# Seven-product down projection: the product of sums first, A11's product in the third bank and copied to two halves, A12's product one step later

## The chip, the cores and the metric

The kernel runs on one core of a Trainium2 chip. The metric is the device time of one execution in microseconds (us), as the median of several runs; lower is better. Before the change it is 731.59 us, the median of three runs (731.53 to 734.29).

The engines are named as in the profile: PE (TensorE, the matmuls), PEld (its weight loads, which run beside the matmuls), DVE (VectorE), ACT (ScalarE), POOL (GpSimd), SP (SyncE, which issues nearly all DMAs). Matmuls write into PSUM, eight banks of 128 partitions by 512 float32; ACT and DVE read the banks.

## The reference

```python
def _L0_cond_ref(x, cond, norm_w, up_w, down_w):      # x (4, 1024, 512), FF = 2048
    scale = cond @ norm_w.T + 1.0
    ms = jnp.mean(x * x, axis=-1, keepdims=True)
    h = x * (scale[:, None, :] * jax.lax.rsqrt(ms + EPS))
    u = h @ up_w.T                                     # (4, 1024, 4096)
    val, gate = jnp.split(u, 2, axis=-1)
    h = val * jax.nn.gelu(gate, approximate=False)
    hq = h + jax.lax.stop_gradient(act_quant(h) - h)   # whole numbers over a scale per token
    wq = down_w + jax.lax.stop_gradient(weight_quant(down_w) - down_w)   # -1, 0, 1 over one scale
    y = hq @ wq.T                                      # the down projection
    return y + x
```

The change touches the last product alone, `hq @ wq.T`: per batch element 1024 tokens by 2048 channels against a 2048 by 512 matrix.

## The kernel before

The four elements of the batch (`b`) go through the kernel one after the other. The up projection of an element runs in 16 slots (`slot`, one for each 128 of the 2048 channels); for `b` of 1 to 3 it is done with seven products in place of eight (`product` at L574, six matmuls of 512 columns each, in the PSUM banks A, B and E). In the slots of element `b`, the quantization of element `b - 1` is done on DVE and ACT by a planner (`Filler`) that spreads its pieces over places x, y and z of each slot, and the down projection of `b - 1` is put into the slots `DOWN`, 10 to 13, one *pair* of token tiles in each: tile `a` of the first half of the tokens and tile `a` of the second half. For `b` of 1 and 2 that makes eight pairs. The pairs 0 to 2 of the element 2 are done after the last slots, in the tail (`old_first`, `old_third` and the calls beside them); so there are eleven pairs in all. The fourth of element 2 and all of the last element use the plain `down_mm`.

A pair (`Pair`, L812) is itself a product of two-by-two blocks, by seven block products of eight matmuls each. The left blocks are A11, A12 (tokens of the first half, channels of the lower and upper half) and A21, A22, each 128 by 1024 in bfloat16, in R. The right blocks B11 to B22 and their sums T1 to T4 lie in `wd8` in fp8. The left sums s1 to s4 are made by DVE: s1 in `sum1` (L827), into the H slot that this slot will fill only later, and then in `sums` (L834 to L836): A21 becomes s3, s2 takes A11's place, s4 takes A12's place. Each may only be written when the product that reads the old block is done.

A block product is `Pair.product` (L839): eight matmuls of 256 columns, into one half of a bank. All matmuls of all pairs carry the line L851; one product is told from another by its place in time. A pair uses three banks of the tag `po`, k1, k2 and k3 (in the tail pair 1 has the banks B, A and E instead). In the order of PE's queue a slot with a pair runs:

- `early`: `first`, that is A11 x B11 into the second half of k1, with a first matmul of 512 columns (`both`), which writes both halves with the same numbers; ACT copies the second half onto the first (L859); s1 x T1 into k3; then A12 x B21 accumulates onto k1's first half. Then DVE's `sums`.
- three to four up products (A, E, B, and A of the slot before),
- `third` (place `mid[0]`): s2 x T2 accumulates onto k1's second half, ACT copies that half to k2's second half (L868), and DVE adds k3 to the output rows (L891, `onto`),
- an up product in E, then `fourth`: s4 x B22 onto k1's second half, s3 x T3 onto k2's second half, the copy L877; DVE adds k1 to the rows, and makes the next pair's s1,
- an up product in A, then `fifth`: A22 x T4 onto k2's first half, and the rows go out.

A matmul that accumulates onto what ACT has written needs an earlier matmul to have marked the place as written. A `po_set` matmul at L1381 does this once, for the bank of k2, before the first pair.

The order on every engine is that of the code (a manual schedule). The semaphores are laid by the tile framework from what each instruction reads and writes.

Of the kernel before, what the change touches and what calls it, by code (L numbers as in the profile page):

```python
# [18 lines left out]
P = 128  # L19
# [31 lines left out]
def glu_quant_kernel(  # L51
# [15 lines left out]
    HALF = D // 2  # L67
# [44 lines left out]
    for n in range(0, P, 32):  # L112
        c = slice(n, n + 32)
# [25 lines left out]
    def s_tile(g):  # L139


        if g >= NJ:
            return SXY[:, (g + 1) % 2]
        return S_more if g % 3 == 2 else SXY[:, g % 3]
# [667 lines left out]
    class Pair:  # L812
# [23 lines left out]
            DVE.tensor_tensor(self.s[4], a12, self.s[2], ALU.subtract)  # L836
            self.s[3] = a21

        def product(self, w, name, bank, half, start, stop, both=False):  # L839


            w = w.rearrange("p (j t) -> p j t", t=P)
            t = w_block(name)
            n = NJ // 2
            for j in range(n):
                m, po = t[:, :, j], bank[:, half * HALF : (half + 1) * HALF]
                po = po.rearrange("p (c o) -> p c o", c=2)
                if both and j == 0:
                    m = m.rearrange("p (y c) o -> p y c o", y=1).to_broadcast([P, 2, 2, P])
                    po = bank.rearrange("p (y c o) -> p y c o", y=2, c=2)  # L850
                PE.matmul(  # L851
                    po, w[:, j], m, start=start and j == 0, stop=stop and j == n - 1,
                    skip_group_check=True,
                )

        def first(self, banks):
            self.banks = k1, _, k3 = banks
            self.product(self.part(0, 0), "B11", k1, 1, True, True, True)
            ACT.copy(k1[:, :HALF], k1[:, HALF:])  # L859
            self.product(self.s[1], "T1", k3, 0, True, True)  # L860
            self.product(self.part(0, 1), "B21", k1, 0, False, True)

        def third(self, xrs, dq):

            k1, k2, k3 = self.banks
            self.xrs, self.dq = xrs, dq
            self.product(self.s[2], "T2", k1, 1, False, True)
            ACT.copy(k2[:, HALF:], k1[:, HALF:])  # L868
            for h in range(2):
                self.onto(h, k3[:, :HALF], slice(HALF, D))  # L870

# [405 lines left out]
    for b in range(1, B):  # L1277
        dve, act = Filler(), Filler()
        gains(b)
        am = am_tile(b - 1)  # L1280
        dq = state[b - 1] = sm.tile([P, 2 * NA], F32, name=f"dq_{b}", tag="dq")
        last_pair = NJ // 2 - 1
        for h in range(2):
            add_pair(
                dve, act, b - 1, last_pair, h, (0, "xz"[h]),
                lambda now, h=h: token_max(b - 1, h, am),
            )
        for h in range(2):
            for cost, f in token_scale(h, am):
                dve.add((1, "x"), cost, lambda now, f=f: f())  # L1290
        add_pieces(dve, act, b - 1, am, PIECES, (2, "x"))
        for i in range(NJ // 2 - 1):
            for h in range(2):
                add_pair(dve, act, b, i, h, (2 * i + 3, "x"))
        steps = {}
        pairs = {}
        if b + 1 < B:
            sc = cond_load_scale(b + 1)
            bring = lambda b=b, sc=sc: cond_bring(b + 1, sc)
            steps[1, "z"] = [(bring, (0.4, 0))]  # L1300
            p0 = b * NJ + 12
            plan = [
                (None, p0, ((6, "z"), (7, "x"), (7, "y"), (9, "y"), (10, "x"), (10, "z"))),
                (p0 + 4, None, ((9, "y"), (10, "x"), (10, "y"), (11, "y"), (12, "x"), (12, "x"))),
                (None, None, ((10, "y"), (11, "x"), (11, "y"), (13, "x"), (13, "y"), (13, "z"))),
                (p0 + 2, p0 + 4, ((9, "z"), (12, "x"), (12, "y"), (14, "x"), (14, "y"), (14, "z"))),
            ]
            for a, (at, nx_at, places) in enumerate(plan):
                def make(a=a, at=at, nx_at=nx_at, b=b):
                    toks[a] = Tokens(b + 1, a, at, nx_at)  # L1310
                    toks[a].load()
                fs = [
                    make,
                    lambda a=a: toks[a].norm(),
                    lambda a=a, sc=sc: toks[a].scale(sc),
                    lambda a=a: toks[a].high(),
                    lambda a=a: toks[a].low(DVE),
                    lambda a=a: toks[a].turn(),
                ]
                costs = ((0, 0), (0, 1.6), (0, 1.5), (0, 2.1), (2.6, 0), (0, 0))  # L1320
                for place, f, c in zip(places, fs, costs):
                    steps.setdefault(place, []).append((f, c))
        for j in range(NJ):
            g = b * NJ + j
            down = b + 1 < B and j in DOWN
            if down:
                pair, a = pairs[j], DOWN[j]
                xrs = [down_load(b - 1, h, a) for h in range(2)]
            early_sums, late_sums = D_SUM_AT.get((b, j), ((), ()))
            left = SLOT_US + PAIR_US * down - OWN_US + 0.4  # L1330
            more = D_SUM_US * len(late_sums) + 0.7 * (j + 1 == min(DOWN) and b + 1 < B)
            left -= D_SUM_US * len(early_sums) + more
            mine = {p: [sum(c[e] for _, c in steps.get((j, p), ())) for e in range(2)] for p in "xyz"}
            left -= sum(mine[p][0] for p in "xyz")
            act_left = {"x": 2.7, "y": 2.2 if down else 1.1, "z": 0}

            def run(p):
                nonlocal left
                for f, _ in steps.get((j, p), ()):
                    f()  # L1340
                if p == "x":
                    cap = min(left, 3.9 - mine["x"][0] - (0 if down else mine["y"][0] + more))
                    left -= cap - dve.run((j, p), cap)
                elif p == "z":
                    left = dve.run((j, p), left)
                if p != "z":
                    act.run((j, p), act_left[p] - mine[p][1])

            def early():
                if down:  # L1350
                    pair.first([po_bank(f"po_{b}_{a}_{n}") for n in range(3)])
                    pair.sums()
                d_sums(early_sums)

            def next_pair():
                if b + 1 < B and j + 1 in DOWN:
                    pairs[j + 1] = Pair(b - 1, DOWN[j + 1])
                    pairs[j + 1].sum1(h_slots(g + 1)[:, 0, 0])

            def more_sums():  # L1360
                next_pair()
                d_sums(late_sums)

            mid = [nothing] * 3
            if j + 1 == min(DOWN):
                mid[0] = more_sums
            if down:
                mid = [lambda: (pair.third(xrs, dq), d_sums(late_sums)), lambda: (pair.fourth(), next_pair()), lambda: (loads(), pair.fifth())]

            def loads():  # L1370
                if NJ + 2 <= g + 2 < B * NJ:
                    s_load_x(g + 2)
                if NJ + 2 <= g + 1 < B * NJ:
                    s_load_y(g + 1)


            def late():
                if b == 1 and j + 1 == min(DOWN):

                    banks = [po_bank(f"po_set_{n}") for n in range(3)]  # L1380
                    PE.matmul(  # L1381
                        banks[1].rearrange("p (a t) -> p a t", t=P),
                        s_tile(g + 1)[:, 0, 0, :P], t_view(b)[:, :, 0, 0, 0, :],
                        start=True, stop=True,
                    )

            if b + 1 == B and j in DOWN and DOWN[j] < 3:
                pairs[DOWN[j]] = Pair(b - 1, DOWN[j])
                places = old_places(DOWN[j])
                pairs[DOWN[j]].sum1(places[0])  # L1390
                pairs[DOWN[j]].sums(*places[1:])
            if j == 4:
                token_turn(b - 1, am)
            if j == 5:
                bring_dq = token_undo(b - 1, dq)
            if j == 6:
                bring_dq()
            if j == NJ - 1:
                get_ready()
            elif b == 1 and j == 0:  # L1400
                get_ready()
            slot(g, lambda: run("x"), lambda: run("y"), lambda: run("z"), early, mid, late)
            if not down:
                loads()
        assert not act.items and not dve.items, (b, dve.items, act.items)
# [162 lines left out]
```

## Time and profile before

| | |
|---|---|
| median of three runs | 731.59 us |
| the profiled execution | 730.43 us |
| its span, first to last instruction | 728.6 us |
| PE busy | 719.9 us (99%) |
| DVE busy | 581.2 us (80%) |
| ACT busy | 396.3 us (54%) |
| POOL busy | 196.1 us (27%) |
| granted TensorE clock | 1.000 |
| L851, matmuls in `po` from R | 448 records, mean 275 ns |
| L868, ACT copy of 128x256 | 11, each 357 ns |

The span is what the profiler saw from the first to the last instruction. The run takes 1.8 us more than that, which lies around the program. The records of matmuls are pipelined: a record of 256 columns lasts 0.27 us, though the next matmul starts about 0.11 us after it. So the time of a product on PE is read from one start to the next, not from the lengths of its records.

The pairs lie in three stretches: 274 to 337 us (pairs 0 to 3 of element 0, in the slots 10 to 13 of `b` = 1), 445 to 508 us (element 1, `b` = 2), and 669 to 696 us (the tail).

### The profile page before, as it was taken

What the parts mean: (1) busy time and instruction counts of PE and PEld (TensorE: products, weight loads), DVE (VectorE), ACT (ScalarE), POOL (GpSimd) and SP (SyncE); (2) the same over time, 40 slices, a digit from 0 to 9 for tenths busy, and PEclk for the clock granted to TensorE, in tenths of its full rate; (3) what the DMA queues carried; (4) which work ended last, traced back from release to release, by engine and by line L of the source; (5) the groups of instructions that cost most, each with busy time, mean ns of one, the idle gap of its engine ahead of it and who ended that gap; (6) DMA issues with size and microseconds to landing.
All of it is one profiled execution on the core that took longest, in us unless ns stands there. A gap on an engine that the chain in (4) does not pass through costs nothing.

```text
span 728.6 us, 10140 instructions
## 1 busy us (share of the span) xinstructions
PE 719.9 (99%) x3661; PEld 358.8 (49%) x3661; DVE 581.2 (80%) x819; ACT 396.3 (54%) x629; POOL 196.1 (27%) x207
## 2 busy tenths in 40 slices
PE   7999999999999999999999999999999999999998
PEld 3544444444444446655444445665444444445744
DVE  7877889975698899788689897787678888755897
ACT  6868876772336674444335676543433665332274
POOL 1379887775100033440000030360020000000100
PEclk9999999999999999999999999999999999999999
DMA  6759999988444654876735646866934555452253
GB/s 236 251 172 303 291 273 249 254 199 230 117 102 102 131 155 130 180 186 159 181 101 103 131 101 174 202 144 163 230 96 102 90 114 104 101 102 89 89 188 115
DMA packets 203982, 117.30 MB, mean 161 GB/s; under 512 B 165382, under 2 KB 174487, under 8 KB 203932
## 3 DMA queue, kind: packets, MB, share of 16 engines
q1 hardware_dynamic: 203642, 116.33, 63.8%
q8 instruction: 28, 0.46, 0.2%
q10 hardware_dynamic: 290, 0.33, 0.1%
q14 instruction: 22, 0.18, 0.1%
HBM read 54.22 MB, written 23.09 MB: 106 GB/s over the span
## 4 chain that ended last, share of the span: by engine, by line
PE 96%; DVE 1%; DMA 1%; ACT 0%; issue 0%; SPq 0%; DVEq 0%
PE A L580 34%; PE E L580 17%; PE pg L595 10%; PE pv L595 10%; PE B L580 9%; PE po L851 8%; PE po_end L800 4%; PE po L800 1%; DMA H<-in_x_dram 1%; DMA SXY<-H 1%; PE po_B L851 0%; PE ptx L941 0%; PE pv L638 0%; DVE R L949 0%; PE pw L323 0%; PE pg L638 0%
## 5 line engine op out<-in xcount | busy, mean ns | idle before, releaser
L580 PEld LDWEIGHTS <-SXY 128*128 128x128 f16 x2016 | 197.2, 98 | 232.3 <-issue 0.6
L580 PE MATMUL A<-R,SXY 128*128 128x512 f16 x1152 | 266.2, 379 | 0.0
L580 PE MATMUL E<-R,SXY 128*128 128x512 f16 x576 | 140.0, 379 | 0.1
L678 DVE SCALAR_TENSOR_TENSOR H<-A,sg,t 128x512 f32<-128x512 f32 x48 | 36.0, 750 | 73.4 <-PE A L580 73.2
L730 POOL PARTITION_ALL_REDUCE am<-R x8 | 14.4, 1794 | 230.7 <-DVE R L716 230.7
L772 DVE TENSOR_TENSOR H<-H,am 128x1024 f32<-128x1024 f32 x64 | 76.2, 1216 | 0.0
L595 PEld LDWEIGHTS <-SXY 128*128 128x128 f16 x486 | 47.5, 98 | 57.4 <-DMA SXY<-H 0.8
L691 ACT ACTIVATE t<-t,sg 128x512 f32<-128x512 f32 x48 | 34.6, 721 | 70.1 <-DVE t L688 69.9
L580 PE MATMUL B<-R,SXY 128*128 128x512 f16 x288 | 70.0, 379 | 0.0
L714 DVE TENSOR_REDUCE gm<-H 128x512 f32<-128x1024 f32 x56 | 69.0, 1232 | 1.0
L595 PE MATMUL pg<-R,SXY 128*128 128x512 f16 x252 | 57.8, 379 | 0.3 <-DMA SXY<-H 0.3
L851 PE MATMUL po<-wd,R 128*128 128x256 fp8e4 (+1 forms) x448 | 56.8, 275 | 0.0
L595 PE MATMUL pv<-R,SXY 128*128 128x512 f16 x234 | 54.4, 379 | 0.0
L851 PEld LDWEIGHTS <-R 128*128 128x128 bf16 (+1 forms) x480 | 47.0, 98 | 12.8
L675 ACT ACTIVATE t<-B,sg 128x512 f32<-128x512 f32 x48 | 33.0, 688 | 36.4 <-PE B L580 36.4
L484 POOL TENSOR_SCALAR ssq<-ssq 128x2 f32<-128x2 f32 x12 | 3.6, 299 | 176.8 <-ACT xt L514 124.1
L658 ACT COPY t<-A 128x512 f32<-128x512 f32 x48 | 28.0, 583 | 39.5 <-PE A L580 39.2
L666 ACT COPY B<-A 128x512 f32<-128x512 f32 x48 | 27.4, 572 | 39.0 <-PE A L580 38.6
L780 ACT ACTIVATE H<-H 128x1024 f32<-128x1024 f32 x38 | 39.9, 1050 | 14.1 <-DVE H L772 14.1
L670 ACT COPY v<-E 128x512 f32<-128x512 f32 x48 | 28.1, 586 | 31.3 <-PE E L580 27.8
L716 DVE TENSOR_TENSOR R<-R,gm 128x512 f32<-128x512 f32 x56 | 41.9, 749 | 1.3
L697 DVE SCALAR_TENSOR_TENSOR H<-v,sg,t 128x512 f32<-128x512 f32 x48 | 36.6, 762 | 7.4 <-ACT t L691 7.4
(207 smaller groups left out, 972.5 us busy)
## 6 DMA issues: line engine op xcount, KB each, us to landing
SXY<-s_dram SPq DMA_DIRECT2D x57, 256.0 KB, 3.2
s_dram<-SXY SPq DMA_DIRECT2D x18, 384.0 KB, 3.3
H<-in_L_cond_up_w_dram SPq DMA_DIRECT2D x13, 512.0 KB, 5.6
SXY<-s_dram SPq DMA_DIRECT2D x39, 128.0 KB, 3.3
xr<-in_x_dram SPq DMA_DIRECT2D x19, 256.0 KB, 3.5
out_dram<-xr SPq DMA_DIRECT2D x19, 256.0 KB, 2.6
H<-in_x_dram SPq DMA_DIRECT2D x8, 512.0 KB, 7.9
R<-in_L_cond_down_w_dram SPq DMA_DIRECT2D x8, 512.0 KB, 7.1
```

Of the source, the lines that this page charges most:

```text
L580: PE.matmul(o, s[:, w, k, :], tv[:, :, c, l, k, :], start=start and n == 0, stop=stop and n == len(TERMS) - 1, skip_group_check=True,)
L595: PE.matmul(ps, a[k // 2][:, w, k % 2, :], XP[:, l, k, h * TOK : (h + 1) * TOK], start=n == 0, stop=n == len(terms) - 1,)
L675: ACT.activation(cur["t1"], pb, AF.Gelu, scale=gain(g, 1))
L678: DVE.scalar_tensor_tensor(h_half(g - 1, 0), prev["A"], gain(g - 1, 0), prev["t1"], ALU.mult, ALU.mult)
L691: ACT.activation(prev["t2"], prev["t2"], AF.Gelu, scale=gain(g - 1, 1))
L697: DVE.scalar_tensor_tensor(h_half(g - 1, 1), prev["v"], gain(g - 1, 0), prev["t2"], ALU.mult, ALU.mult)
L714: DVE.tensor_reduce(gm[0], v, AX.X, ALU.max, apply_absolute_value=True)
L716: return [largest, lambda: DVE.tensor_tensor(m, m, gm[0], ALU.max)]
L772: DVE.tensor_tensor(v, v, r.to_broadcast([P, 2, TOK]), ALU.mult)
L780: ACT.activation(v, v, AF.Copy, bias=MAGIC)
L800: PE.matmul(po.rearrange("p (y c o) -> p y c o", c=2, o=P), q[:, a, h, j], wd8[:, :, j // n, j % n, :, y0:y1].rearrange("p c o y -> p y c o"),
L851: PE.matmul(po, w[:, j], m, start=start and j == 0, stop=stop and j == n - 1, skip_group_check=True,)
```

## The change

`first` makes s1 x T1 first, into k3's first half. Then A11 x B11 goes into k3's second half, which was not used before, with eight matmuls of 256 columns; `both` and its wide matmul are gone. One ACT copy, now of 512 columns, reads this half twice and writes both halves of k1. A12 x B21 leaves `first` and is put in `third`, after s2 x T2 and the copy to k2. As A12 is then still needed when `sums` runs, s4 goes to the other half of the H slot that holds s1 (the tail's pairs had places of their own for their sums already). Before the first pair the `po_set` matmul is done for two banks in place of one.

```diff
-        def product(self, w, name, bank, half, start, stop, both=False):
+        def product(self, w, name, bank, half, start, stop):
...
-                if both and j == 0:
-                    m = m.rearrange("p (y c) o -> p y c o", y=1).to_broadcast([P, 2, 2, P])
-                    po = bank.rearrange("p (y c o) -> p y c o", y=2, c=2)
...
         def first(self, banks):
             self.banks = k1, _, k3 = banks
-            self.product(self.part(0, 0), "B11", k1, 1, True, True, True)
-            ACT.copy(k1[:, :HALF], k1[:, HALF:])
             self.product(self.s[1], "T1", k3, 0, True, True)
-            self.product(self.part(0, 1), "B21", k1, 0, False, True)
+            self.product(self.part(0, 0), "B11", k3, 1, True, True)
+            m1 = k3[:, HALF:].rearrange("p (y o) -> p y o", y=1).to_broadcast([P, 2, HALF])
+            ACT.copy(k1.rearrange("p (y o) -> p y o", y=2), m1)
...
             self.product(self.s[2], "T2", k1, 1, False, True)
             ACT.copy(k2[:, HALF:], k1[:, HALF:])
+            self.product(self.part(0, 1), "B21", k1, 0, False, True)
...
-                    pair.sums()
+                    pair.sums(None, h_slots(g)[:, 0, 1])
...
-                    PE.matmul(
-                        banks[1].rearrange("p (a t) -> p a t", t=P),
-                        s_tile(g + 1)[:, 0, 0, :P], t_view(b)[:, :, 0, 0, 0, :],
-                        start=True, stop=True,
-                    )
+                    for bank in banks[:2]:
+                        PE.matmul(
+                            bank.rearrange("p (a t) -> p a t", t=P),
+                            s_tile(g + 1)[:, 0, 0, :P], t_view(b)[:, :, 0, 0, 0, :],
+                            start=True, stop=True,
+                        )
```

## The prediction

> **What bounds the kernel now.** I read the page first, then who waited for whom, then the timeline around the pairs.
>
> ```profile
> PE 719.9 (99%) x3661; PEld 358.8 (49%) x3661; DVE 581.2 (80%) x819; ACT 396.3 (54%) x629; POOL 196.1 (27%) x207
> ...
> PE 96%; DVE 1%; DMA 1%; ACT 0%; issue 0%; SPq 0%; DVEq 0%
> ```
>
> The second line is the chain that ended last: 96% of the span is PE's queue running one matmul after another. A 99% busy PE alone would prove little, as records overlap. So I took starts: between 264 us and the end only three matmuls start later than their queue would let them, two by 0.2 us (a product in E, 265.7 and 436.8 us) and one in a pair:
>
> ```profile
> PE po L851 <- DVE H L827: 0.6, 1, 0.6
> ```
>
> (who waited for whom, PE alone: total, times, longest). Hence whatever is added to PE's stream in the pairs is added to the end, and whatever is taken out is gained, with hardly any idle time on PE to absorb either.
>
> **The wide matmul (removed).** The first pair, timeline (start us, us, engine, line, operation):
>
> ```profile
> 273.86 0.38 PE L1381 MATMUL po_set<-R,SXY 128*128 128x512 f16 x1
> ...
> 274.07 1.14 PE L851 MATMUL po<-wd,R 128*128 128x512 fp8e4 x8
> ...
> 275.06 1.04 PE L851 MATMUL po<-wd,H 128*128 128x256 fp8e4 x8
> 275.26 0.36 ACT L859 COPY po<-po 128x256 f32<-128x256 f32 x1
> ...
> 275.93 1.04 PE L851 MATMUL po<-wd,R 128*128 128x256 fp8e4 x8
> ```
>
> A11's eight matmuls, one of them wide, take 275.06 - 274.07 = 0.99 us; s1's eight narrow ones 275.93 - 275.06 = 0.87. The change makes the first like the second: -0.11 us (the wide one's extra 256 columns), eleven times, -1.2 us. The second `po_set` costs what the first does: 274.07 - 273.86 = +0.2 us, once.
>
> **The wait that is removed.** A12 x B21 now waits in `first` for the copy L859. Here that copy ends at 275.62 and B21 starts at 275.93, exactly 0.87 after s1's product: the wait is hidden by s1's product and costs nothing. In no pair but one (below) does `first` take longer than its columns. So nothing is gained here. DVE's s4 no longer waits for B21 either; DVE (80%) sets no end, so this is worth nothing by itself.
>
> **The wait that is added.** B21 now stands in PE's queue right behind s2 x T2 and writes k1's first half, while ACT reads k1's second half for the copy to k2. The changed program, as built, lets B21's first matmul in each of the eleven pairs wait for that very copy: the framework keeps two engines apart by bank, though the halves differ. Before, PE went on into bank E:
>
> ```profile
> 283.28 1.04 PE L851 MATMUL po<-wd,R 128*128 128x256 fp8e4 x8
> ...
> 284.15 1.46 PE L580 MATMUL E<-R,SXY 128*128 128x512 f16 x6
> 284.35 0.36 ACT L868 COPY po<-po 128x256 f32<-128x256 f32 x1 [0.29 <-PE po L851]
> ```
>
> From T2's first matmul to the copy's end is 284.71 - 283.28 = 1.43 us; the same in the other pairs I read (298.56 to 299.99, 313.85 to 315.28, 329.90 to 331.33), 1.48 in the tail (673.32 to 674.80). From ACT's end to a matmul that waits for it: at 16.39 us ACT's L349 ends, the load and matmul of L638 start at 16.45, so 0.06. Before, the next matmul came 0.87 after T2's first. The added wait is 1.43 + 0.06 - 0.87 = 0.62 us in a slot, 1.48 + 0.06 - 0.87 = 0.67 in the tail. This supposes that ACT is free when T2 ends. The line view of L868 says so for all eleven copies:
>
> ```profile
>   PE po L851: 6.1, 10
>   PE po_B L851: 0.5, 1
> ```
>
> (what ACT sat idle for before the copy: us, times). So 8 x 0.62 + 3 x 0.67 = **+7.0 us**. Behind the waiting matmul stand B21's other seven, the product in E, then B22 and T3; DVE's sum of E and ACT's Gelu behind them slide with PE. As nothing in PE's queue may pass, nothing covers this. Its lower bound is 0.56 a pair (no hand-over time at all), its upper bound what a late ACT would add; the least idle time before L868 was 0.28 us, so none here.
>
> The Trainium skill ("PSUM — Partial Sum Buffer", section "PSUM bank collisions raise a hardware error") speaks against this step: PSUM is to be guarded by bank and 32-partition quadrant, not by address, since PE's write and another engine's access to one bank at once is an error even at different columns. No row of before shows PE writing into a bank that ACT is reading, so the trace cannot decide it. By the rule the wait is needed and the sum is as below; were halves independent, the 7.0 would drop out.
>
> **s1's product comes first.** T1 now opens the slot, 0.99 us earlier than before, and needs DVE's s1. Two slots show where that matters:
>
> ```profile
> 304.40 1.13 DVE L827 TENSOR_TENSOR H<-R 128x1024 bf16<-128x1024 bf16 x1
> ...
> 305.62 1.04 PE L851 MATMUL po<-wd,H 128*128 128x256 fp8e4 x8
> ```
>
> ```profile
> 319.93 1.14 PE L851 MATMUL po<-wd,R 128*128 128x512 fp8e4 x8
> ...
> 320.40 1.20 DVE L827 TENSOR_TENSOR H<-R 128x1024 bf16<-128x1024 bf16 x1
> ...
> 321.66 1.05 PE L851 MATMUL po<-wd,H 128*128 128x256 fp8e4 x8 [0.59 <-DVE H L827]
> ```
>
> In the third pair s1 ends at 305.53, just ahead of T1, but the slot begins at 305.62 - 0.98 = 304.64: T1 placed first would wait 0.89 + 0.05 (hand-over, from 321.61 to 321.66) = 0.94. The seventh pair (slot at 475.53, s1 ready at 476.41) gives 0.93. The fourth waits 0.74 now and would wait 1.73. The other pairs have their s1 at least 0.4 us ahead of their slot. Against these stand PE's own delays: by the third pair PE is late by 0.2 + 2 x (0.62 - 0.11) = 1.2 us. DVE's chain to s1 slides by only part of that: it waits at 302.75 for a row load that the SP queue issues behind loads paced by PE about a slot earlier (some 0.7 late by then). That leaves 0.94 - (1.2 - 0.7) = 0.4. In the seventh, without the `po_set`, by the same difference, 0.4 too. In the fourth DVE works with no gap over 0.11 us from 304.40 to 321.61, so s1 comes 0.7 late while PE's slip has grown to 1.2 + 0.4 + 0.5 = 2.1: 1.73 + 0.7 - 2.1 = 0.3 in place of 0.74. Sum +0.4 + 0.4 - 0.4 = **+0.4 us**. Bounds: s1 does not slide at all and all these waits vanish, -0.74; s1 slides fully with PE, 0.94 + 0.93 + 0.99 = +2.9.
>
> **The rest.** The copy in `first` grows from 357 ns to that of a 512-column copy (L666, 572 ns), +0.2 us of ACT; it ends some 0.6 us after A11's product, and ACT's next task waits for an up product of 1.29 us. Without that cover it would be 0.2 us a pair, 2.4 us. s4's write to H is the same 692 ns DVE operation. SP's queue keeps its order and its waits; one POOL sum waits for a product of the batch before, long done. DVE's first `onto` gains a wait for the copy in `first`, done 5 us earlier. All these: 0.
>
> **Sum.** -1.2 + 0.2 + 7.0 + 0.4 = **+6.4 us** (bounds -1.2 + 0.2 + 11 x 0.56 - 0.7 = +4.5, and -1.0 + 7.0 + 2.9 = +8.9). The profiled execution took 730.43 (span 728.6), so 736.8 by it; the median, 1.2 higher, gives 731.59 + 6.4 = 738.0. Which base the next runs have, I can't know; I take 737.7.
>
> **Rivals.**
> - *s1 slides fully with PE* (each T1 wait is paid whole, +8.9): 740.5. For it: DVE is paced by PE in most slots. Against: hardly a gap on DVE before the fourth pair's s1, which alone takes back 0.7.
> - *B21 does not really wait, faster than before.* The price of the wait is the whole loss. If matmuls into the other half went ahead beside the copy, only -1.0 + 0.4 = -0.6 remains: 731.0; with vanishing T1 waits 729.9. It decides below (1.0 - 0.4) / 11 = 0.05 us of wait a pair. For it: the halves share no column. Against: the built program's wait, and no ACT copy that could end before T2 does.
> - *DVE's freed time pays back.* Its s4 wait goes, its s1 comes earlier, the 0.74 and both 0.2 waits vanish: +7.0 - 1.0 - 0.7 - 0.4 = +4.9, 736.5. It is inside the likeliest's range.
>
> **Chances.** The forecast 0.80 (its own range 735 to 739), full slide 0.13, B21 without a wait 0.05, something else 0.02. The range is 734.9 (730.43 + 4.5) to 740.5. A change of 0.5% is 3.7 us, about what a measurement can tell from none; forecast and full slide lie over it: slower 0.93, within 0.5% 0.05, faster 0.02.
>
> **What would show it.** In the profile after, a wait of PE at L848's matmuls for ACT's L865 copy, eleven times, some 6 to 7 us in all, with 1.5 us from T2's first matmul to B21's first; T1 behind s1 in the third, fourth and seventh pair; no 512-column matmul in the pairs. If PE's starts there are 0.87 apart, the forecast is wrong; if the time is over 741, ACT or DVE has fallen behind as well.

## The result, and the profile after

The changed kernel takes 738.22 us (median of six runs, 736.76 to 740.01) against 731.59 us (six runs, 730.97 to 734.29): the ratio is 1.008, with a 95% interval of 1.0057 to 1.0104. It is 0.8% slower. A second set, taken beside the experiments, gave 737.43 against 731.53 us, ratio 1.0084 (1.0071 to 1.0097).

The profiled execution took 738.60 us with a span of 736.8, so 8.2 us more span than before. From its page, the busy times and the chain that ended last:

```profile
PE 721.8 (98%) x3662; PEld 360.4 (49%) x3662; DVE 580.1 (79%) x819; ACT 399.5 (54%) x629; POOL 195.8 (27%) x207
...
PE 89%; DVE 7%; DMA 1%; ACT 1%; issue 1%; SPq 0%; ACTq 0%; DVEq 0%
```

PE has still 98% of the span, and no share tells that something is wrong. The waits of PE from 264 us to the end do (who waited for whom: total us, times, longest; in the changed kernel the matmuls of the pairs carry L848, the copy to k2 L865 and s1 L827):

```profile
PE po L848 <- ACT po L865: 4.6, 10, 0.5
PE po_B L848 <- ACT po_A L865: 0.5, 1, 0.5
PE po L848 <- DVE H L827: 0.3, 1, 0.3
```

Before, the same view had one line, that for s1, with 0.6. The two new lines are the eleven waits of A12 x B21 for the copy to k2. They look smaller here (5.1 us) than they are: idle time is counted from the modelled end of the last record, 0.27 us after its start, while the next matmul could have started 0.11 us after it. The timeline of the first pair's third step has the whole price:

```profile
285.15 1.04 PE L848 MATMUL po<-wd,R 128*128 128x256 fp8e4 x8
...
286.23 0.36 ACT L865 COPY po<-po 128x256 f32<-128x256 f32 x1 [0.29 <-PE po L848]
...
286.63 1.03 PE L848 MATMUL po<-wd,R 128*128 128x256 fp8e4 x8 [0.44 <-ACT po L865]
...
287.50 0.38 PE L580 MATMUL E<-R,SXY 128*128 128x512 f16 x1
```

From T2's first matmul to B21's first it is 286.63 - 285.15 = 1.48 us, where a product takes 0.87 (287.50 - 286.63): 0.61 lost. PE waits for ACT, and ACT had waited for PE: neither is slow, each stands until the other has handed over.

The fall of PE's share of the chain from 96% to 89% means less than it seems. The chain of waits of the changed kernel goes from T1's wait in the fourth pair (0.3 us) back to s1, and from there stays on DVE, which had hardly a gap, back to 308.75 us. One short wait puts 16 us under another engine's name.

**Where the 8.2 us are.** To keep apart what the pairs do from what the start does, I cut each profile at four matmuls: the first `po_set`, the first of the fifth pair, the first of the tail's pairs, and the last of all. The differences of their starts are the stretches of this table (us).

| kernel | first four pairs | next four | tail | sum | against before |
|---|---|---|---|---|---|
| before | 171.10 | 224.31 | 55.74 | 451.15 | |
| before, once more | 171.09 | 224.31 | 55.73 | 451.13 | -0.02 |
| changed | 172.98 | 226.31 | 57.37 | 456.66 | +5.51 |
| changed, once more | 173.03 | 226.30 | 57.37 | 456.70 | +5.55 |
| B21 ahead of T2 | 171.07 | 224.83 | 55.39 | 451.29 | +0.14 |
| the same, B11 first | 171.05 | 223.96 | 55.39 | 450.40 | -0.75 |
| before, B21 behind the copy | 172.76 | 226.73 | 57.69 | 457.18 | +6.03 |
| changed, copy twice | 174.37 | 227.85 | 58.54 | 460.76 | +9.61 |
| T1 between copy and B21 | 170.67 | 223.88 | 55.98 | 450.53 | -0.62 |
| before, B21 ahead of T2 | 171.02 | 224.31 | 55.71 | 451.04 | -0.11 |
| all covered | 170.12 | 223.88 | 55.39 | 449.39 | -1.76 |

Two profiles of one kernel agree here to 0.05 us in every stretch, where whole times of it scatter by 3 to 5. The sum of the changed kernel is 5.5 us longer. The other 2.6 us of its span lie before 188 us, in code that the change does not touch (the last section). The second profile of before is that of a single run (730.67 us).

### The profile page after: what moved, and what is told of

The parts are those of the page before. It is cut to its first block, busy times and chain, and to the rows that moved or that the text cites. A ratio compares the mean times of both kernels' runs of the same rounds, so it can differ in the third digit from the quotient of the medians.

```text
span 736.8 us, 10143 instructions
## 1 busy us (share of the span) xinstructions
PE 721.8 (98%) x3662; PEld 360.4 (49%) x3662; DVE 580.1 (79%) x819; ACT 399.5 (54%) x629; POOL 195.8 (27%) x207
## 4 chain that ended last, share of the span: by engine, by line
PE 89%; DVE 7%; DMA 1%; ACT 1%; issue 1%; SPq 0%; ACTq 0%; DVEq 0%
PE A L580 31%; PE E L580 16%; PE pg L595 10%; PE pv L595 10%; PE B L580 8%; PE po L848 8%; PE po_end L800 4%; DVE gm L714 1%; DVE R L716 1%; PE po L800 1%; DMA H<-in_x_dram 1%; PE ptx L939 1%; DVE R L709 1%; DMA SXY<-H 1%; DVE H L678 0%
## 5 line engine op out<-in xcount | busy, mean ns | idle before, releaser
L848 PE MATMUL po<-wd,R 128*128 128x256 fp8e4 x384 | 49.7, 272 | 4.6 <-ACT po L865 4.6
L848 PEld LDWEIGHTS <-R 128*128 128x128 bf16 (+1 forms) x416 | 40.6, 98 | 15.3 <-issue 7.0
L716 DVE TENSOR_TENSOR R<-R,gm 128x512 f32<-128x512 f32 x56 | 42.7, 762 | 1.3
```

Source lines behind the costliest of these rows:

```text
L716: return [largest, lambda: DVE.tensor_tensor(m, m, gm[0], ALU.max)]
L848: PE.matmul(po, w[:, j], m, start=start and j == 0, stop=stop and j == n - 1, skip_group_check=True,)
```

## The experiments

**The changed kernel once more.**

> The changed kernel once more, unchanged, beside the runs that follow. In its profile the eleven waits of A12 x B21 for the copy to k2 sum to 6.9 us and T1 waits for s1 in the fourth pair only (0.4 us); so the pairs cost 5.6 us more than before, and the 2.6 us by which the first profile's start was longer were chance. If so, the ratio to before is 1.007 to 1.009 and its pairs' stretches are again 1.9, 2.0 and 1.7 us longer than before. The rival (the change also makes the start longer, by other code or by other loads) wants the first po_set matmul at 276 us again, not at 274.

737.43 us (four runs), ratio 1.0084 (1.0071 to 1.0097). The stretches repeat. Its first `po_set` is at 275.54 us, between the two forecasts; the kernel with the copy twice, the same code up to there, has it at 273.99. So the changed kernel's code can begin early too; the last section has the starts of all profiles.

**B21 ahead of T2.**

```diff
-            self.product(self.s[2], "T2", k1, 1, False, True)
-            ACT.copy(k2[:, HALF:], k1[:, HALF:])
             self.product(self.part(0, 1), "B21", k1, 0, False, True)
+            self.product(self.s[2], "T2", k1, 1, False, True)
+            ACT.copy(k2[:, HALF:], k1[:, HALF:])
```

> The changed kernel with A12 x B21 ahead of s2 x T2 in the third step, so that it no longer stands behind the copy to k2. Theory (the wait for that copy is the loss): the eleven waits, 6.9 us, are gone, which leaves -1.2 + 0.2 and the waits of T1 for s1. These come back where PE is no longer late: up to 0.94 in the third pair, 0.9 in the fourth in place of 0.74, 0.9 in the seventh, +2.0 in all; 730.6 to 732.6, ratio 0.999 to 1.001. Rival (the loss lies in T1 placed first, the longer copy or s4's new place): it stays at 737 to 738.

731.28 us (twelve runs), ratio 0.9997 (0.9981 to 1.0013): the loss is gone with one product moved ahead of two lines. No wait for the copy is left, and T1's waits for s1 are back, as they must be when PE is no longer late; the timeline of the third pair:

```profile
307.32 1.04 PE L848 MATMUL po<-wd,R 128*128 128x256 fp8e4 x8
307.98 1.10 DVE L827 TENSOR_TENSOR H<-R 128x1024 bf16<-128x1024 bf16 x1
309.14 0.44 PEld L848 LDWEIGHTS <-H 128*128 128x128 bf16 x5 [1.06 <-DVE H L827]
309.14 0.61 PE L848 MATMUL po<-wd,H 128*128 128x256 fp8e4 x4 [0.78 <-DVE H L827]
```

T1 could start at 307.32 + 0.87 = 308.19 and starts at 309.14, 0.95 late; 0.94 in the seventh pair. In the fourth it does not wait at all (0.9 was expected). PE is 0.85 us late there, as expected; but s1 ends 1.4 us earlier than before, counted from the first `po_set`. It began 1.1 earlier, as DVE's L716 ahead of it took 0.69 us in place of 1.75, and took 0.97 in place of 1.20.

**The same, B11 first.**

```diff
-            self.product(self.s[1], "T1", k3, 0, True, True)
             self.product(self.part(0, 0), "B11", k3, 1, True, True)
+            self.product(self.s[1], "T1", k3, 0, True, True)
```

> As the run before, and A11 x B11 put ahead of s1 x T1 in the first step, both still in k3. Then s1 is needed 0.87 us later than with T1 first. Theory: no wait for the copy to k2, T1 waits only in the fourth pair (0.7 to 0.9 us), 1.2 saved by the narrow matmuls, 0.2 paid for po_set: 730.4 to 730.8 against 731.6, ratio 0.9985 to 0.999. If T1's place was worth nothing, it equals the run before it. If the longer copy or s4's place costs, it is above 1.000.

731.09 us (twelve runs), ratio 0.999 (0.9978 to 1.0002). The times alone do not tell this from no change; the stretches do, with 450.40 against 451.15. The view has one wait of T1 left, 0.83 us in the fourth pair; in the third and the seventh T1 starts 0.07 late each, too little for the view. So s1 x T1 in first place costs 0.9 us here (451.29 - 450.40), which is what its waits differ by (1.89 - 0.97). The longer copy and s4's new place, still in this kernel, cost nothing that shows: -1.0 and 0.97 - 0.75 of wait make -0.78, measured -0.75.

**The kernel before, B21 behind the copy.**

```diff
             self.product(self.s[1], "T1", k3, 0, True, True)
-            self.product(self.part(0, 1), "B21", k1, 0, False, True)
...
             ACT.copy(k2[:, HALF:], k1[:, HALF:])
+            self.product(self.part(0, 1), "B21", k1, 0, False, True)
...
-                    pair.sums()
+                    pair.sums(None, h_slots(g)[:, 0, 1])
```

> The kernel before, with its wide matmul, its copy and its order in the first step, but A12 x B21 moved behind s2 x T2 and the copy to k2, and s4 in the other half of the H slot, as it must be then. Theory (the move alone makes the loss): eleven waits of 0.6 us, 6.9 us, minus up to 0.7 where T1's wait in the fourth pair is covered by PE's lateness: 737.8 to 738.5, ratio 1.0085 to 1.0095. Rival (the move costs nothing, the loss is T1 first or the new copy): 731.6, ratio 1.000.

736.94 us (six runs), ratio 1.0086 (1.007 to 1.0103). This is the old kernel, with its wide matmul and its first step, and the one move gives the whole loss. Its waits of PE from 264 us on:

```profile
PE po L851 <- ACT po L867: 4.6, 10, 0.5
PE po_B L851 <- ACT po_A L867: 0.5, 1, 0.5
```

They are those of the changed kernel. T1's wait for s1 has gone, covered by PE's lateness, so the stretches make 6.86 - 0.75 = 6.1; measured 6.03.

**The kernel before, B21 ahead of T2.** As the last one, with B21 put before T2 in the third step.

> The kernel before, with its wide matmul and its first step, but A12 x B21 moved into the third step ahead of s2 x T2, and s4 in the H slot. It differs from the run with B21 behind the copy by one thing, the order of B21 against T2 and the copy. Theory: no wait for the copy, T1's wait in the fourth pair stays 0.7; 0.0 against before, ratio 0.999 to 1.001, and 6.0 us less than with B21 behind. Rival (moving B21 out of the first step, or s4's new place, costs): above 1.003.

731.63 us (twelve runs), ratio 1.0003 (0.9991 to 1.0015). The move itself is free; where B21 stands against the copy is worth 457.18 - 451.04 = 6.1 us.

**The copy twice.**

```diff
             ACT.copy(k2[:, HALF:], k1[:, HALF:])
+            ACT.copy(k2[:, HALF:], k1[:, HALF:])
             self.product(self.part(0, 1), "B21", k1, 0, False, True)
```

> The changed kernel with the copy to k2 done twice, so that A12 x B21 waits for both. Theory (PE stands still until ACT has ended, nothing covers it): each of the eleven waits grows by one copy of 0.36 us less the overlap of two copies in a row on ACT (0.1), 0.26 to 0.36 us; 2.9 to 3.9 us over the changed kernel, 740.5 to 741.5, ratio to before 1.012 to 1.014. Rival (the wait is hidden or is not ACT's): no longer than the changed kernel, 737.5.

740.19 us (four runs), ratio 1.0128 (1.01 to 1.0157). The first pair's third step:

```profile
283.72 0.36 ACT L865 COPY po<-po 128x256 f32<-128x256 f32 x1 [0.29 <-PE po L848]
284.11 0.36 ACT L866 COPY po<-po 128x256 f32<-128x256 f32 x1
...
284.51 0.71 PE L848 MATMUL po<-wd,R 128*128 128x256 fp8e4 x5 [0.83 <-ACT po L866]
```

Each wait is 0.39 us longer (from one matmul's start to the next it is 1.105 us in place of 0.717), which is the second copy with its gap, 284.11 - 283.72. I had expected 0.26 to 0.36, as two ACT instructions often overlap by 0.1 in the profile; these do not. The stretches grew by 4.1, against 11 x 0.39 = 4.3 less T1's shorter waits.

**T1 between the copy and B21.**

```diff
             ACT.copy(k2[:, HALF:], k1[:, HALF:])
+            self.product(self.s[1], "T1", k3, 0, True, True)
             self.product(self.part(0, 1), "B21", k1, 0, False, True)
```

(T1 leaves the first step.)

> The changed kernel with s1 x T1 moved out of the first step to stand between the copy to k2 and A12 x B21 in the third. The semaphore wait of B21 stays as it is; what changes is that PE has 0.87 us of work in another bank before it. The wait needs 0.61 us (0.67 in the tail), so theory: no PE wait is left for the copy, and none of T1 for s1 either, as s1 now has half a slot more. -1.2 + 0.2 - 0.7 = -1.7 against before: 729.8 against 731.5, ratio 0.9975 to 0.998. Rival (the loss comes with B21 following T2 in the same bank, covered or not): 735 or more.

730.54 us (twelve runs), ratio 0.9985 (0.9971 to 0.9999). The third step of the first pair, T2, copy, T1, B21:

```profile
282.83 0.93 PE L848 MATMUL po<-wd,R 128*128 128x256 fp8e4 x7
...
283.60 1.04 PE L848 MATMUL po<-wd,H 128*128 128x256 fp8e4 x8
283.80 0.36 ACT L864 COPY po<-po 128x256 f32<-128x256 f32 x1 [0.29 <-PE po L848]
...
284.47 1.04 PE L848 MATMUL po<-wd,R 128*128 128x256 fp8e4 x8
```

B21 starts 0.87 after T1, with nothing to wait for: the copy ended at 284.16. The order "B21 after T2 and the copy" is unchanged, and so is what it waits for; only the cover is new. So it is exposure that costs. But the expected -1.7 came out as -0.62. The waits of PE from 264 us on say why:

```profile
PE A L580 <- DVE v L694: 0.4, 1, 0.4
PE po L848 <- DVE R L835: 0.4, 1, 0.4
```

With only one product left in `first`, T2 reaches s2 too early in the third pair, and in the tail the up product in A reaches its bank before DVE has read it. Start to start these two cost 0.54 and 0.59 us, together the 1.1 by which the stretches miss the -1.7.

**All covered.** In the slots T1, then B21, then T2 and the copy in the third step; in the tail T1 stays in the first step.

```diff
-            self.product(self.s[1], "T1", k3, 0, True, True)
+            if self.b == B - 2:
+                self.product(self.s[1], "T1", k3, 0, True, True)
...
+            if self.b < B - 2:
+                self.product(self.s[1], "T1", k3, 0, True, True)
+            self.product(self.part(0, 1), "B21", k1, 0, False, True)
             self.product(self.s[2], "T2", k1, 1, False, True)
             ACT.copy(k2[:, HALF:], k1[:, HALF:])
-            self.product(self.part(0, 1), "B21", k1, 0, False, True)
```

> The changed kernel with no exposed wait left in the pairs: in the slots s1 x T1 and then A12 x B21 stand ahead of s2 x T2 in the third step, in the tail T1 stays in the first step and only B21 moves ahead of T2. Theory (narrow matmuls -1.2, second po_set +0.2, T1's old wait for s1 -0.7, nothing else): from the first po_set to the last matmul 449.4 us against 451.1 before and 456.7 in the changed kernel; ratio to before 0.997 to 0.998. Rival (some stall always comes back, as T2 behind s2 and A behind v did when T1 stood behind the copy): 450.4 to 451.1, ratio 0.999 to 1.000.

729.82 us (eleven runs) against 731.91, ratio 0.9972 (0.996 to 0.9984): faster than both kernels. From 264 us to the end the view of PE's waits is empty. The first pair's third step runs through:

```profile
281.71 1.04 PE L848 MATMUL po<-wd,H 128*128 128x256 fp8e4 x8
...
282.58 1.80 PE L848 MATMUL po<-wd,R 128*128 128x256 fp8e4 x15
```

The stretches are 449.39 us, 1.76 less than before, which is the sum of the saved columns (-1.2), the second `po_set` (+0.2) and T1's old wait (-0.75). So the narrow first product and the third bank's free half are worth what the prediction said, and the longer copy costs nothing; the changed kernel paid 6.85 us for one product's place.

Not tried: B21 without its wait beside the copy. PE and ACT would then be in one bank at once with nothing to order them.

## Why the prediction was right, step by step

- **What bounds the kernel.** PE's queue. Every experiment's time follows from PE's starts alone; 6.1 us of wait on PE came out as 6.0 us of stretch.
- **The wide matmul, -1.2 us, and the second `po_set`, +0.2.** The changed kernel's first pair (timeline):

```profile
276.50 0.59 PE L1380 MATMUL po_set<-R,SXY 128*128 128x512 f16 x2
...
276.93 1.04 PE L848 MATMUL po<-wd,H 128*128 128x256 fp8e4 x8
```

  Two `po_set` take 0.43, and every product of the pairs is 0.87 apart. Shown as a sum by the last experiment.
- **The removed wait is worth nothing.** Right: the kernel before with B21 ahead of T2, which has no such wait either, gains 0.1 us.
- **The added wait, +7.0 us.** Measured 8 x (0.717 - 0.109) + 3 x (0.772 - 0.109) = 6.85. The hand-over from ACT to PE was 0.04 (286.59 to 286.63), not 0.06. The line view of the copy counts all eleven as waiting for PE (4.5 us over ten, 0.5 over one), and all eleven as waited for by it; so ACT was never late, as supposed. The rule of the Trainium skill ("PSUM — Partial Sum Buffer", section "PSUM bank collisions raise a hardware error"), that PSUM is to be guarded by bank and quadrant and not by address, is not tested here: the built program keeps the two engines apart by bank, and the runs show the price of that. That two engines in the halves of one bank would collide no run here shows.
- **s1's product first, +0.4 us.** This term was mis-sized: it was -0.33. In the third and seventh pair T1 did not wait, in the fourth 0.42 in place of 0.75; so T1 stood behind s1 in one of the three pairs named. PE's lateness was as worked out (1.2 us at the third pair). The wrong step is "that leaves 0.94 - (1.2 - 0.7) = 0.4": I let s1's end slide with its chain. Its start slid by 0.3, and then it took less time, 0.68 us for the 1.13 of before:

```profile
306.08 1.28 POOL L527 TENSOR_TENSOR xn<-xn,sc 128x512 f32<-128x512 f32 x1
...
307.35 0.68 DVE L827 TENSOR_TENSOR H<-R 128x1024 bf16<-128x1024 bf16 x1
...
307.44 1.18 POOL L535 TENSOR_TENSOR xt<-xn 128x256 f32<-128x256 f32 x1
```

  Less the 2.6 us of the longer start, s1 ended 0.1 us earlier than before although PE was 1.2 us later. With PE on time (B21 ahead of T2) T1 waits the whole 0.95, as the 0.94 worked out for it.

  What the sum left out is POOL. Here its L527 ended (306.08 + 1.28 = 307.36) as s1 began. In the seventh pair of before it was under way:

```profile
474.58 1.28 POOL L527 TENSOR_TENSOR xn<-xn,sc 128x512 f32<-128x512 f32 x1
474.77 1.65 DVE L827 TENSOR_TENSOR H<-R 128x1024 bf16<-128x1024 bf16 x1
```

  L527 ended at 475.86, and s1 about 0.55 later. The eleven profiles have 121 records of s1. In 58 no POOL instruction was under way when s1 began, and s1 took 0.68 to 0.69 us. In 58 a POOL instruction had 0.24 to 1.24 us left, and s1 ended 0.54 to 0.55 after it. In the other five it had under 0.1 left, and s1 took 0.68. So in these profiles a start of s1 under a POOL instruction settles its end by that instruction and not by DVE's chain: in the third pair s1 ends 31.7 us after the first `po_set` in six of the eleven profiles, though it begins anywhere from 29.9 to 30.7. No run moves POOL's work on purpose, so this rests on the match of the times.

  In the fourth pair two misses all but cancel: s1 came 0.40 late (0.7 in the forecast) and PE 1.7 (2.1), so 1.73 + 0.40 - 1.7 = 0.43.
- **The sum.** The stretches say -1.2 + 0.2 + 6.85 - 0.33 = 5.5 where the forecast had 6.4. The medians differ by 6.6 and, in the second set, 5.9; in the profiles what varies beside the stretches is the start. The forecast of 737.7 lies 0.5 below the first median and 0.3 above the second. That it came so near is in part luck: its sum was 0.9 too high, and the starts in the first set of the changed kernel were, by the estimate in the last section, about 1.1 later than those of before.
- **The rivals.** Full slide (740.5) and B21 without a wait (731.0) did not come. That DVE's freed time pays back (+4.9) held for a part of T1's old wait, not for the two waits in E, which stayed at 0.2.

## What to carry to other kernels

When a product is moved behind a copy, ask which bank the copy reads and which bank the product writes; if they are one, the product waits, in this program, for the whole round trip, although its columns differ. The wait costs nothing when the product is put ahead of the copy, or when enough matmuls into another bank stand between the two (0.87 us of them here, for waits of 0.61 and 0.66); so look for an order before you look for a faster copy. Where whole times scatter by more than the effect, cut the profiles at the same instructions and compare the stretches. And before a DVE sum is moved, see what POOL does when it begins: here that changed its time from 0.68 to 1.65 us.

## What the runs showed that was not expected

**The start varies by 3.5 us with the same code.** Up to the first `po_set` all these kernels run the same instructions, yet the up projection in seven products begins at 185.6 us in the profile before, 188.2 in the changed one, 187.3 in its second run, 185.7 with the copy twice, and 189.1 with B21 ahead of T2. The four profiles of kernels with the old first step all begin between 185.6 and 185.9; of the seven with the new one two begin at 185.7, the others at 186.7 to 189.1. So the profiles alone do not clear the change. The other runs say more. If in every run of a kernel the stretches and what follows them are as in its profile (an estimate), its median leaves 275.0 to 275.3 us to the first `po_set` for before, 276.1 and 275.3 for the two sets of the changed kernel, and 274.0 to 275.3 for the others; a single run of before (735.1 us) comes to 278.5. A longer start is thus not bound to the change.

The first 30 us of three of them (window, busy us of each engine, PEclk, DMA share, GB/s): before, changed, B21 ahead of T2:

```profile
0.00:30.00 30.00, 25.83 (x128) 13.38 (x129) 23.67 (x85) 21.03 (x44) 8.68 (x15) 1.00 0.81 276
```

```profile
0.00:30.00 30.00, 24.28 (x113) 13.36 (x114) 21.07 (x82) 19.37 (x42) 7.12 (x14) 0.94 0.74 253
```

```profile
0.00:30.00 30.00, 24.77 (x109) 13.06 (x110) 20.42 (x81) 18.57 (x40) 6.29 (x12) 0.89 0.69 243
```

The granted clock is 1.00, 0.94 and 0.89, and in the changed kernel PE had stood for 2.8 us waiting for the first tokens just before:

```profile
11.57 3.30 PE L939 MATMUL ptx<-ident,H 128*128 128x128 f32 x16 [2.78 <-DVE H L934]
```

Before, this wait was 1.5 us and the clock stayed at 1.00. But the length of the wait does not decide it alone: it was 2.5 us with B21 ahead of T2, where the clock is 0.89, and 2.5 us in the second run of the changed kernel, where it is 1.00. What does decide it stays open.

**s1 took 0.68 to 1.79 us for the same 1024 elements.** One kernel shows nearly the whole range: in the seventh pair of before s1 took 1.65 us in one profile and 0.68 in the other, where POOL had 0.07 us left as s1 began; in that of the changed kernel 0.68 and 1.00. The L716 of the run with B21 ahead of T2 goes the same way: 0.69 us where it began ahead of POOL's instruction, and 1.75 before, where it began under one and ended 0.55 after it.
